# A local-attention stage with its steps in another order, TensorE steps of one tile mode side by side

## The chip, the cores and the metric

The kernel runs on one core of one Trainium2 chip, in float32 (a few tiles of zeros apart). The metric is the device time of one execution in microseconds. A core has five engines, each with its own queue that it works through in order: TensorE (PE; its weight loads are shown apart as PEld), VectorE (DVE), ScalarE (ACT), GpSimd (POOL) and SyncE (SP), which issues the DMAs here. Engines wait for each other by semaphores.

## The reference

Two blocks with adaptive layer norm follow each other on x of 16 x 256 x 128. The first has full attention with 16 heads of 8, and a six-layer local-attention transformer as its second half. The other has a state-space layer and a linear layer. The change is in the six layers:

```python
def attn_layer(x, Wqkv, qs, ksc, Wo):
    qkv = x @ Wqkv
    q, k, v = jnp.split(qkv, 3, -1)
    q, k, v = (sh(q), sh(k), sh(v))          # 16 heads of 64
    q = l2norm(q) * qs
    k = l2norm(k) * ksc
    q = q * cos * scale + rotate_half(q) * sin * scale
    k = k * cos * inv + rotate_half(k) * sin * inv
    out = local_attention(q, k, v)           # windows of 32: own and previous one
    return out @ Wo

def ffn_layer(x, g, bln, W1, b1, W2, b2):
    xn = (x - mu) / jnp.sqrt(var + 1e-05) * g + bln
    a, gate = jnp.split(xn @ W1 + b1, 2, -1)
    return a * jax.nn.gelu(gate, approximate=False) @ W2 + b2

for i in range(DEPTH):                       # 6
    x = attn_layer(shift_tokens(x), Wqkv[i], q_scale[i], k_scale[i], Wo[i]) + x
    x = ffn_layer(shift_tokens(x), ln_g[i], ln_b[i], W1[i], b1[i], W2[i], b2[i]) + x
```

## The kernel before

The kernel has three stages: full attention (about 0 to 431 us), the six layers (431 to 3332 us) and the state-space block with the linear layer (to the end). x is kept transposed, features on partitions, in F.

In the middle stage a group is two sequences (512 tokens); eight groups make one layer and 48 groups the stage. `run` (class `Transformer`) works in 48 periods. In each it goes through ORDER, a list written out by hand of step names with a lag: `Tk10@1` is step T for k, sequence 1, token half 0, of the group that entered one period ago. So up to four groups are in work at once. The list's order is the order of the instructions in each engine's queue, since the stage is recorded under a manual schedule: nothing reorders it. After the 48 periods TAIL does the rest of the last groups, with some steps of the next stage's first group among them (marked `@s`).

The steps, with their engine and, for PE, the tile of the array that the weights take (rows * columns):

- P (L628, PE 128*128): q or k of 128 tokens for all heads, two matmuls of 512 columns. Q (ACT) squares them, C and N (DVE) multiply by cosine and sine, R (DVE) sums the squares, A (POOL) adds the two rotary parts, MXS (POOL), SQ (ACT), RR (DVE) make the norms' inverses, M (POOL) applies them.
- T (L702, PE 64*128): transposes q or k, 16 matmuls of 64 columns. E (ACT) copies the result out.
- K (ACT) writes the mask into PSUM, S (L759, PE 64*32) adds the scores: 64 small float32 products, 128 matmul records and as many weight loads in the profile.
- MX, SB (DVE) find and subtract the maxima, EX (ACT) takes exponentials, SM (DVE) their sums, NR (POOL) divides, TP (DVE) transposes.
- X (PE 128*128), W (ACT), V (SP, two DMAs) lay out x for the values. G (L817, PE 32*128) multiplies the probabilities with x; B (ACT) copies it to `at`, two copies a G.
- Y (L838, PE 128*128): four heads a step through the product of value and output weights. FADD (DVE) adds the result to F.
- F1, F5 (PE transposes), F2 (DVE), F3, FN (POOL), F4, F6 (ACT) are the layer norm; FP (L914, PE), FE (ACT), FM (DVE), FY (L938, PE), FF (DVE) the feed-forward part.
- `value_output` (L608, PE, 64-row weights) makes the product of value and output weights of the next layer, in the last two periods of a layer, and copies it on ACT.

PSUM is handed out by `Slots`: `two` has three places of two banks (P, T, K with S, G twice, FP, the value product), `one` has two places (X, Y, F1, F5, FY). A step that takes a place waits until all that used it before have let it go: a P's place is free after two Q, one C and two N; that of K and S after SB; that of T after E; that of G after B. Other Slots hold the SBUF buffers (`u` seven, `w` four, `pp`, `pT`, `qT` two each). Places go round in the order in which the list frees them.

Of the kernel before, what the change touches and what calls it, by code (L numbers as in the profile page):

```python
# [17 lines left out]
P = 128  # L18
B, S, D = 16, 256, 128
# [3 lines left out]
NG = B // G  # L23
# [435 lines left out]


ORDER = """
Pq00@0 FM2@3 Cq00@0 Nq000@0 EX01@1 Mq10@1 Mk10@1 SM01@1 EX00@1 G10@2 Qq000@0 FADD0@2 B101@2 B100@2
Ak11@1 FY@3 Nq001@0 Aq00@0 SM00@1 Qq001@0 Rq00@0 G11@2 B111@2 FF@3 Mq11@1 X0@1 Pk01@0 Ck01@0 Tk10@1
B110@2 Pq01@0 Nk010@0 Nk011@0 W0@1 Ek10@1 Qk010@0 Cq01@0 Qk011@0 Pk00@0 Ak01@0 Tq10@1 V0@1 Qk000@0
Qk001@0 Nq010@0 Nq011@0 Aq01@0 NR00@1 Y10@2 Eq10@1 Y11@2 Qq010@0 Qq011@0 Rk01@0 Rk00@0 NR01@1 Ck00@0
K10@1 Nk000@0 Rq01@0 MXS0@0 Mk11@1 Tq11@1 Eq11@1 S10@1 Nk001@0 TP00@1 Ak00@0 Pq11@0 MX10@1 SB10@1
SQ0@0 Qq110@0 Nq110@0 Nq111@0 Cq11@0 Pq10@0 Qq100@0 Qq101@0 Tk11@1 Y12@2 Qq111@0 Nq100@0 Nq101@0
Cq10@0 Ek11@1 Y13@2 FADD1@2 G00@1 K11@1 B000@1 S11@1 TP01@1 B001@1 X1@1 G01@1 RR0@0 EX10@1 Aq10@0
MX11@1 Mk00@0 SB11@1 F1@2 F2@2 B010@1 B011@1 Mq00@0 W1@1 EX11@1 Rq10@0 Mq01@0 Pk10@0 Pk11@0 Qk110@0
Tk00@0 Ek00@0 F3@2 FN@2 F4@2 Ck10@0 Nk100@0 Nk101@0 Ck11@0 Aq11@0 V1@1 Y00@1 Tq00@0 Eq00@0 Y01@1  # L470
Tq01@0 F5@2 Qk100@0 Y02@1 Qk101@0 K00@0 SM11@1 F6@2 Mk01@0 SM10@1 S00@0 Eq01@0 Tk01@0 Rk10@0 Nk110@0
Nk111@0 NR11@1 TP11@1 Qk111@0 MX00@0 SB00@0 Ek01@0 FP0@2 FE0@2 Rk11@0 K01@0 FP1@2 NR10@1 Y03@1
Rq11@0 MXS1@0 FE1@2 FM0@2 FM1@2 Ak10@0 SQ1@0 TP10@1 RR1@0 S01@0 MX01@0 FP2@2 FE2@2 SB01@0
"""

TAIL = """
Ak11@0 Mk10@0 X0@0 FADD0@1 Mk11@0 W0@0 G10@1 FM2@2 L1@s B101@1 Mq11@0 G11@1 EX00@0 B110@1 B111@1  # L480
ST@s B100@1 Mq10@0 FY@2 Tq11@0 AG@s Tk10@0 Tk11@0 SM00@0 Eq11@0 Tq10@0 FF@2 Ek10@0 RS@s NB@s Y10@1
K11@0 Ek11@0 EX01@0 Y11@1 NR00@0 S11@0 V0@0 TP00@0 Y12@1 Eq10@0 SM01@0 MX11@0 Y13@1 XN@s L2@s SB11@0
K10@0 G00@0 FADD1@1 X1@0 EX11@0 SM11@0 S10@0 HT@s NR01@0 F1@1 B001@0 TP01@0 MX10@0 SB10@0 B000@0
NR11@0 W1@0 PX1@s U1@s G01@0 B010@0 PX0@s F2@1 B011@0 TP11@0 V1@0 Y00@0 F3@1 EX10@0 FN@1 Y01@0 G11@0
U0@s SM10@0 Y02@0 NR10@0 TP10@0 F4@1 Y03@0 PD@s B111@0 B110@0 XD@s WB@s G10@0 B100@0 B101@0 PZ1@s
F5@1 FADD0@0 ZA1@s F6@1 PZ0@s ZA0@s EE@s WW@s Y10@0 W2@s Y11@0 Y12@0 Y13@0 ZR1@s FADD1@0 FP0@1 F1@0
ZR0@s FP1@1 LL@s FP2@1 FE1@1 LW@s F2@0 FE0@1 F3@0 ZF@s FM1@1 FM0@1 FE2@1 FN@0 DU@s F4@0 FM2@1 F5@0
FY@1 F6@0 FP1@0 FP2@0 FP0@0 FE1@0 FF@1 FE2@0 TB@s FM1@0 FM2@0 FE0@0 FM0@0 FY@0 CB@s FF@0 MS@s
"""


# [20 lines left out]
class Transformer:  # L512
# [460 lines left out]
    def run(self):  # L973
        steps = []
        for o in ORDER.split():
            name, lag = o.split("@")
            base = name.rstrip("0123456789") if name[0] != "F" or name[:2] == "FA" else name
            steps.append((name, int(lag)))
        last = max(lag for _, lag in steps)
        groups = {}  # L980
        n = DEPTH * NG
        for jh in range(2):
            self.value_output(0, jh)
        for p in range(n):
# [722 lines left out]
```

## Time and profile before

| what | value |
|---|---|
| median of 3 runs | 3852.29 us (3850.81 to 3856.6) |
| the profiled execution's span | 3847.4 us, 4.9 below the median |
| mean granted TensorE clock | 0.987 |
| first stage, 0 to 431 us | PE 379, DVE 229, ACT 220, POOL 105 us busy |
| 500 to 3200 us | PE 2668, weight loads 1626, DVE 2548, ACT 2052, POOL 1981 us busy |
| 3330 us to the end | PE 478, DVE 463, ACT 430, POOL 410 us busy |
| matmuls, weight loads | 45040, 45040 |

The profile is of one execution. Its span runs from the first to the last instruction of the program; the profiled execution's own time is given by that span alone, and what lies around it is seen only as the 4.9 us by which the median of the runs is longer. Busy times overlap within an engine by a little, since one instruction's end covers the next one's start; for PE the ends are modelled, so that start to next start tells more than a length.

### The profile page before, as it was taken

The page shows a single profiled execution, that of the slowest core. Times are in us where ns is not written, and L with a number is a line of the kernel's source. Part 1 is how long each engine was busy: PE and PEld are TensorE (multiplying, and loading weights), DVE is VectorE, ACT ScalarE, POOL GpSimd, SP SyncE. Part 2 cuts the span into 40 slices and gives each one's busy share as a digit, 9 for nine tenths or more (in the row PEclk, how much of TensorE's full clock was granted, in tenths as well). Part 3 has the DMA queues.
Part 4 walks back from the last instruction along what each step waited for, and adds up shares of the span by engine and source line. Part 5 has one row for each costly group of instructions (what it writes and reads, how often), then busy time and mean ns, then how long its engine had stood idle before and what let it go on. Part 6 is the DMA issues. An engine that isn't in the chain of part 4 may idle for free.

```text
span 3847.4 us, 104054 instructions
## 1 busy us (share of the span) xinstructions
PE 3693.1 (96%) x45040; PEld 2197.4 (57%) x45040; DVE 3385.9 (88%) x4736; ACT 2820.0 (73%) x4009; POOL 2603.6 (68%) x1636
## 2 busy tenths in 40 slices
PE   8999689999999999999999999999999999899997
PEld 4445355665655656666556656566665556555554
DVE  4665489999999999999999999999999999599997
ACT  3565467777777777777777777777777777689895
POOL 2222477777777777777777777777777776388887
PEclk9999789999999999999999999999999999999999
DMA  1000001000010000100001000010000000243432
GB/s 54 8 7 5 1 7 34 6 5 7 6 34 5 7 6 6 35 6 6 5 7 34 5 6 7 6 34 7 6 6 5 20 7 6 82 117 104 123 109 71
DMA packets 85669, 97.21 MB, mean 25 GB/s; under 512 B 9416, under 2 KB 56668, under 8 KB 84444
## 3 DMA queue, kind: packets, MB, share of 16 engines
q1 hardware_dynamic: 85212, 90.56, 8.5%
q8 instruction: 355, 5.82, 0.6%
q14 instruction: 102, 0.84, 0.1%
HBM read 75.32 MB, written 3.94 MB: 21 GB/s over the span
## 4 chain that ended last, share of the span: by engine, by line
PE 65%; DVE 20%; issue 2%; POOL 1%; ACT 1%; DVEq 0%; POOLq 0%; ACTq 0%
PE py L838 16%; PE pq L628 11%; PE pa L817 7%; PE fp L914 7%; PE s L759 6%; PE pt L702 5%; DVE w L656 3%; PE y L1361 3%; DVE u L644 3%; DVE ss L668 3%; PE db L1345 2%; DVE sm L791 2%; DVE s L1351 2%; PE px L1202 1%; DVE F L951 1%
## 5 line engine op out<-in xcount | busy, mean ns | idle before, releaser
L675 POOL TENSOR_TENSOR u<-u,w 128x1024 f32<-128x1024 f32 x384 | 907.2, 2367 | 405.2 <-DVE w L656 218.3
L690 POOL TENSOR_TENSOR u<-u,r 128x1024 f32<-128x1024 f32 x384 | 724.5, 1903 | 19.1 <-DVE r L686 16.6
L838 PE MATMUL py<-at,wvo 128*128 128x256 f32 x3072 | 736.5, 388 | 0.1
L628 PE MATMUL pq<-wqk,F 128*128 128x512 f32 x1536 | 715.6, 604 | 9.4 <-ACT sq L638 3.3
L638 ACT ACTIVATE sq<-pq 128x512 f32<-128x512 f32 x768 | 432.8, 601 | 301.3 <-PE pq L628 157.3
L838 PEld LDWEIGHTS py<-at,wvo 128*128 128x128 f32 x3072 | 569.6, 192 | 103.2 <-issue 23.2
L644 DVE TENSOR_TENSOR u<-pq,cosl 128x1024 f32<-128x1024 f32 x384 | 466.6, 1215 | 46.2 <-PE pq L628 43.1
L656 DVE TENSOR_TENSOR w<-pq,sinl 128x512 f32<-128x512 f32 x768 | 499.4, 681 | 8.9 <-ACT sq L638 2.1
L828 ACT COPY at<-pa 128x1024 f32<-128x1024 f32 x384 | 368.6, 1012 | 162.9 <-PE pa L817 157.9
L668 DVE TENSOR_REDUCE ss<-sq 128x16 f32<-128x1024 f32 x384 | 451.5, 1196 | 6.2 <-ACT sq L638 6.2
L628 PEld LDWEIGHTS pq<-wqk,F 128*128 128x128 f32 x1536 | 277.0, 191 | 296.2 <-issue 257.2
L817 PE MATMUL pa<-pT,xw 32*128 32x512 f32 x3072 | 411.8, 620 | 5.5 <-ACT sq L638 2.1
L798 POOL TENSOR_TENSOR pp<-pp,sm 128x1024 f32<-128x1024 f32 x192 | 363.8, 1916 | 50.3 <-DVE sm L794 50.3
L702 PEld LDWEIGHTS pt<-ident,u 64*128 64x128 f32 x6144 | 223.7, 139 | 227.0 <-issue 81.8
L1351 DVE TENSOR_TENSOR_SCAN s<-da,db 128x512 f32<-128x512 f32 x256 | 301.1, 1207 | 21.2 <-PE db L1345 9.3
L759 PEld LDWEIGHTS s<-kT,qT 64*32 64x32 f32 x24576 | 257.0, 106 | 90.0 <-issue 79.2
L759 PE MATMUL s<-kT,qT 64*32 64x64 f32 x24576 | 290.3, 227 | 16.4 <-issue 11.3
L702 PE MATMUL pt<-ident,u 64*128 64x64 f32 x6144 | 275.5, 230 | 29.4 <-ACT sq L638 10.6
L772 DVE TENSOR_REDUCE mx<-s 128x16 f32<-128x1024 f32 x192 | 230.5, 1200 | 69.7 <-PE s L759 67.2
L252 DVE TENSOR_REDUCE mx<-s 128x2 f32<-128x512 f32 x256 | 165.3, 687 | 139.9 <-PE sT L280 121.5
L817 PEld LDWEIGHTS pa<-pT,xw 32*128 32x128 f32 x3072 | 180.2, 186 | 172.6 <-issue 76.8
L914 PE MATMUL fp<-hT,w 128*128 128x512 f32 (+1 forms) x576 | 270.7, 606 | 0.0
(223 smaller groups left out, 6269.3 us busy)
## 6 DMA issues: line engine op xcount, KB each, us to landing
btd<-bc SPq DMA_DIRECT2D x72, 512.0 KB
bte<-bc SPq DMA_DIRECT2D x56, 256.0 KB
xw<-xw SPq DMA_DIRECT2D x96, 96.0 KB
wqk<-in_Wqk SPq DMA_DIRECT2D x6, 1024.0 KB
wv<-in_LWvT SPq DMA_DIRECT2D x6, 512.0 KB
wo<-in_Wo SPq DMA_DIRECT2D x6, 512.0 KB
xin<-in_x SPq DMA_DIRECT2D x8, 256.0 KB
out<-ot SPq DMA_DIRECT2D x8, 256.0 KB
```

The costliest lines, as they stand in the source:

```text
L628: nc.tensor.matmul(q.p[:, x], self.F[:, g.b0 + b, o : o + P], g.l.wqk[:, k, x, :], start=True, stop=True)
L638: self.c.nc.scalar.activation(q.sq[:, x], q.p[:, x], AF.Square)
L644: self.c.nc.vector.tensor_tensor(q.u.rearrange("p h x d -> p x h d"), q.p, g.l.cosl[:, t, k].unsqueeze(2).to_broadcast([P, 2, HEADS, DH // ...
L656: self.c.nc.vector.tensor_tensor(q.w[:, :, x], q.p[:, 1 - x], g.l.sinl[:, t, k, x, :].unsqueeze(1).to_broadcast([P, HEADS, DH // 2]), ALU. ...
L668: self.c.nc.vector.tensor_reduce(g.ss[b][:, t, k, :], q.sq.rearrange("p x h d -> p h x d"), AX.XY, ALU.add)
L675: self.c.nc.gpsimd.tensor_tensor(q.u, q.u, q.w, ALU.add)
L690: self.c.nc.gpsimd.tensor_tensor(uf, uf, g.r[b][:, t, k, :].unsqueeze(2).to_broadcast([P, HEADS, DH]), ALU.mult)
L702: self.c.nc.tensor.matmul(q.pt[:, r, j, :], uf[rs, j * P : (j + 1) * P], self.c.ident[rs, rs], is_transpose=True, start=(j == 0), stop=Tru ...
L759: nc.tensor.matmul(s[qs, e, j, :], qT[es, j, qs], kT[es, j, ks : ks + 2 * W], start=False, stop=True, skip_group_check=True,)
L817: self.c.nc.tensor.matmul(g.pa[b, t, w // 2][:, w % 2, :], self.xw[b][qs, t, k, :], g.pT[b, t][qs, k, :], start=(k == 0), stop=(k == 1),)
L838: self.c.nc.tensor.matmul(g.py[b], g.l.wvo[:, h, :], self.at[:, h, :], start=(h == 0), stop=(h == HEADS - 1),)
L914: self.c.nc.tensor.matmul(p[0:n, x, :], g.l.w1[:, w : w + n], g.hT, start=True, stop=True)
```

## The change

ORDER is a new order of the same steps; the cut between two periods is moved (S00, K00, K01, S01 and what follows them now open a period with lag 1 instead of closing it with lag 0). TAIL is new as well; it holds the steps that the moved cut leaves over, and the same early steps of the next stage. `value_output` is split: its matmuls (PW) and its copies (PC) are now steps of the list, where they stood ahead of the list before. Around one period PE's steps change tile mode 29 times in the old order and 21 times in the new one.

PE's steps of the old list, in order: Pq00 G10 FY G11 X0 Pk01 Tk10 Pq01 Pk00 Tq10 Y10 Y11 Tq11 S10 Pq11 Pq10 Tk11 Y12 Y13 G00 S11 X1 G01 F1 Pk10 Pk11 Tk00 Y00 Tq00 Y01 Tq01 F5 Y02 S00 Tk01 FP0 FP1 Y03 S01 FP2.

PE's steps of the new list: S00 S01 FP0 Pq00 Y03 G10 FY Tq10 G11 PW X0 Pk01 Pk00 Pq01 Y10 Tq11 Tk10 Y11 Pq11 Pq10 Y12 S10 Tk11 Y13 G00 S11 F1 X1 G01 Pk10 Tq00 Tq01 Y00 Y01 Tk00 Tk01 F5 Pk11 FP1 FP2 Y02.

```diff
--- before.py
+++ after.py
@@ -459,33 +459,36 @@
 
 
 ORDER = """
-Pq00@0 FM2@3 Cq00@0 Nq000@0 EX01@1 Mq10@1 Mk10@1 SM01@1 EX00@1 G10@2 Qq000@0 FADD0@2 B101@2 B100@2
-Ak11@1 FY@3 Nq001@0 Aq00@0 SM00@1 Qq001@0 Rq00@0 G11@2 B111@2 FF@3 Mq11@1 X0@1 Pk01@0 Ck01@0 Tk10@1
-B110@2 Pq01@0 Nk010@0 Nk011@0 W0@1 Ek10@1 Qk010@0 Cq01@0 Qk011@0 Pk00@0 Ak01@0 Tq10@1 V0@1 Qk000@0
-Qk001@0 Nq010@0 Nq011@0 Aq01@0 NR00@1 Y10@2 Eq10@1 Y11@2 Qq010@0 Qq011@0 Rk01@0 Rk00@0 NR01@1 Ck00@0
-K10@1 Nk000@0 Rq01@0 MXS0@0 Mk11@1 Tq11@1 Eq11@1 S10@1 Nk001@0 TP00@1 Ak00@0 Pq11@0 MX10@1 SB10@1
-SQ0@0 Qq110@0 Nq110@0 Nq111@0 Cq11@0 Pq10@0 Qq100@0 Qq101@0 Tk11@1 Y12@2 Qq111@0 Nq100@0 Nq101@0
-Cq10@0 Ek11@1 Y13@2 FADD1@2 G00@1 K11@1 B000@1 S11@1 TP01@1 B001@1 X1@1 G01@1 RR0@0 EX10@1 Aq10@0
-MX11@1 Mk00@0 SB11@1 F1@2 F2@2 B010@1 B011@1 Mq00@0 W1@1 EX11@1 Rq10@0 Mq01@0 Pk10@0 Pk11@0 Qk110@0
-Tk00@0 Ek00@0 F3@2 FN@2 F4@2 Ck10@0 Nk100@0 Nk101@0 Ck11@0 Aq11@0 V1@1 Y00@1 Tq00@0 Eq00@0 Y01@1
-Tq01@0 F5@2 Qk100@0 Y02@1 Qk101@0 K00@0 SM11@1 F6@2 Mk01@0 SM10@1 S00@0 Eq01@0 Tk01@0 Rk10@0 Nk110@0
-Nk111@0 NR11@1 TP11@1 Qk111@0 MX00@0 SB00@0 Ek01@0 FP0@2 FE0@2 Rk11@0 K01@0 FP1@2 NR10@1 Y03@1
-Rq11@0 MXS1@0 FE1@2 FM0@2 FM1@2 Ak10@0 SQ1@0 TP10@1 RR1@0 S01@0 MX01@0 FP2@2 FE2@2 SB01@0
+K00@1 K01@1 TP11@2 Aq10@1 Rk11@1 FE2@3 MXS1@1 FM2@3 S00@1 S01@1 SQ1@1 Ak10@1 MX00@1 SB00@1 FP0@3
+Pq00@0 MX01@1 FE0@3 RR1@1 EX00@1 FM0@3 Y03@2 SB01@1 EX01@1 SM00@1 Qq000@0 Mq10@1 G10@2 Nq000@0
+Nq001@0 NR00@1 Cq00@0 B101@2 Qq001@0 B100@2 FY@3 Tq10@1 G11@2 SM01@1 Rq00@0 Eq10@1 FADD0@2 FF@3
+B110@2 Ak11@1 TP00@1 PW@0 X0@1 B111@2 Pk01@0 Pk00@0 Ck01@0 Aq00@0 PC@0 W0@1 Mk10@1 Nk010@0 Pq01@0
+Y10@2 Qk000@0 Nk011@0 Mq11@1 Nk000@0 Qk010@0 Qk011@0 Mk11@1 Ck00@0 Qk001@0 Tq11@1 Nk001@0 Tk10@1
+Cq01@0 Rk01@0 Eq11@1 Qq010@0 Ak01@0 Nq010@0 Ek10@1 NR01@1 Rk00@0 Y11@2 Pq11@0 Pq10@0 Y12@2 Nq011@0
+Qq011@0 Qq110@0 K10@1 Rq01@0 Ak00@0 Cq11@0 Aq01@0 Nq110@0 Nq111@0 V0@1 Cq10@0 S10@1 MXS0@0 Nq100@0
+MX10@1 SQ0@0 Qq111@0 Qq100@0 Tk11@1 Nq101@0 Qq101@0 Y13@2 Ek11@1 SB10@1 RR0@0 G00@1 K11@1 S11@1
+FADD1@2 F1@2 B001@1 B000@1 X1@1 TP01@1 EX10@1 MX11@1 SB11@1 Aq11@0 F2@2 G01@1 Mq01@0 B011@1 Pk10@0
+W1@1 Rq10@0 B010@1 Qk100@0 Qk101@0 Mq00@0 V1@1 Mk00@0 Tq00@0 F3@2 SM10@1 Nk100@0 Tq01@0 FN@2 Rk10@0
+EX11@1 Mk01@0 Eq01@0 Eq00@0 Y00@1 Nk101@0 F4@2 Y01@1 Tk00@0 Tk01@0 Ck10@0 Rq11@0 Ek00@0 NR10@1 F5@2
+SM11@1 Pk11@0 F6@2 FP1@2 TP10@1 Ek01@0 NR11@1 Qk110@0 Nk110@0 Ck11@0 FE1@2 FP2@2 FM1@2 Y02@1 Qk111@0
+Nk111@0
 """
 
 
 
 
 TAIL = """
-Ak11@0 Mk10@0 X0@0 FADD0@1 Mk11@0 W0@0 G10@1 FM2@2 L1@s B101@1 Mq11@0 G11@1 EX00@0 B110@1 B111@1
-ST@s B100@1 Mq10@0 FY@2 Tq11@0 AG@s Tk10@0 Tk11@0 SM00@0 Eq11@0 Tq10@0 FF@2 Ek10@0 RS@s NB@s Y10@1
-K11@0 Ek11@0 EX01@0 Y11@1 NR00@0 S11@0 V0@0 TP00@0 Y12@1 Eq10@0 SM01@0 MX11@0 Y13@1 XN@s L2@s SB11@0
-K10@0 G00@0 FADD1@1 X1@0 EX11@0 SM11@0 S10@0 HT@s NR01@0 F1@1 B001@0 TP01@0 MX10@0 SB10@0 B000@0
-NR11@0 W1@0 PX1@s U1@s G01@0 B010@0 PX0@s F2@1 B011@0 TP11@0 V1@0 Y00@0 F3@1 EX10@0 FN@1 Y01@0 G11@0
-U0@s SM10@0 Y02@0 NR10@0 TP10@0 F4@1 Y03@0 PD@s B111@0 B110@0 XD@s WB@s G10@0 B100@0 B101@0 PZ1@s
-F5@1 FADD0@0 ZA1@s F6@1 PZ0@s ZA0@s EE@s WW@s Y10@0 W2@s Y11@0 Y12@0 Y13@0 ZR1@s FADD1@0 FP0@1 F1@0
-ZR0@s FP1@1 LL@s FP2@1 FE1@1 LW@s F2@0 FE0@1 F3@0 ZF@s FM1@1 FM0@1 FE2@1 FN@0 DU@s F4@0 FM2@1 F5@0
-FY@1 F6@0 FP1@0 FP2@0 FP0@0 FE1@0 FF@1 FE2@0 TB@s FM1@0 FM2@0 FE0@0 FM0@0 FY@0 CB@s FF@0 MS@s
+L1@s TP11@1 FE2@2 FM2@2 K00@0 ST@s AG@s Ak10@0 Ak11@0 S00@0 MX00@0 SB00@0 RS@s NB@s K01@0 S01@0 XN@s
+MX01@0 SB01@0 Y03@1 G10@1 B100@1 L2@s HT@s FADD0@1 B101@1 FP0@2 Rk11@0 PX1@s PX0@s FE0@2 MXS1@0
+SQ1@0 U1@s FM0@2 RR1@0 Mk10@0 X0@0 W0@0 U0@s G11@1 B110@1 X1@0 Aq10@0 Mq10@0 W1@0 PD@s B111@1 XD@s
+Tk10@0 Ek10@0 Tq10@0 EX01@0 SM01@0 PZ0@s ZA0@s ZR0@s Mk11@0 PZ1@s ZA1@s Y10@1 Y11@1 Y12@1 Mq11@0
+V0@0 NR01@0 ZR1@s EX00@0 SM00@0 NR00@0 Eq10@0 K10@0 Tk11@0 Ek11@0 Tq11@0 Eq11@0 TP01@0 S10@0 TB@s
+G01@0 TP00@0 Y13@1 MX10@0 CB@s V1@0 FY@2 SB10@0 EX10@0 B011@0 WB@s FADD1@1 B010@0 K11@0 G00@0 B000@0
+S11@0 B001@0 F1@1 SM10@0 FF@2 Y00@0 Y01@0 EE@s MX11@0 NR10@0 TP10@0 SB11@0 EX11@0 F2@1 Y02@0 Y03@0
+WW@s LL@s SM11@0 F3@1 FN@1 F4@1 G10@0 B100@0 F5@1 W2@s F6@1 NR11@0 TP11@0 B101@0 G11@0 B110@0 LW@s
+FP2@1 ZF@s B111@0 Y10@0 Y11@0 Y12@0 DU@s MS@s FE2@1 FM2@1 FADD0@0 Y13@0 FP0@1 FE0@1 FADD1@0 F1@0
+F2@0 F3@0 FP1@1 FM0@1 FE1@1 FM1@1 FY@1 FN@0 F4@0 F5@0 F6@0 FP2@0 FP1@0 FE1@0 FF@1 FM1@0 FE2@0 FP0@0
+FE0@0 FM2@0 FM0@0 FY@0 FF@0
 """
 
 
@@ -599,7 +602,7 @@
         nc, l = self.c.nc, self.layers[i]
         if jh == 0:
             l.wvo = self.wp.tile([P, HEADS, D], F32, tag="wvo", name="wvo")
-        pw = self.two.take([P, 2, 4, D], "pw")
+        pw = l.pw = self.two.take([P, 2, 4, D], "pw")
         for j in range(4):
             for e in range(2):
                 es = slice(e * DH, (e + 1) * DH)
@@ -613,6 +616,11 @@
                     stop=True,
                     skip_group_check=True,
                 )
+
+    def value_output_copy(self, i, jh):
+
+        nc, l = self.c.nc, self.layers[i]
+        pw = l.pw
         for e in range(2):
             o = e * PAIRS + jh * 4
             nc.scalar.copy(l.wvo[:, o : o + 4, :], pw[:, e])
@@ -981,17 +989,20 @@
         n = DEPTH * NG
         for jh in range(2):
             self.value_output(0, jh)
+            self.value_output_copy(0, jh)
         for p in range(n):
             i, j = divmod(p, NG)
             if j == last + 1 and i + 1 < DEPTH:
                 self.load(i + 1)
-            if j >= NG - 2 and i + 1 < DEPTH:
-                self.value_output(i + 1, j - NG + 2)
             if p == n - 4:
                 self.early.load()
             groups[p] = self.group(p)
             for name, lag in steps:
-                if p >= lag:
+                if name in ("PW", "PC"):
+                    if j >= NG - 2 and i + 1 < DEPTH:
+                        value = self.value_output if name == "PW" else self.value_output_copy
+                        value(i + 1, j - NG + 2)
+                elif p >= lag:
                     self.step(name, groups[p - lag])
             groups.pop(p - last, None)
         for o in TAIL.split():
```

## The prediction, made before the run

> **What bounds the kernel now.** I read the engines' shares first, then a stretch of about one period, then TensorE's own timeline, then the waits.
>
> ```profile
> PE 3693.1 (96%) x45040; PEld 2197.4 (57%) x45040; DVE 3385.9 (88%) x4736; ACT 2820.0 (73%) x4009; POOL 2603.6 (68%) x1636
> PE   8999689999999999999999999999999999899997
> DVE  4665489999999999999999999999999999599997
> ```
> ```profile
> 1380.00:1438.20 58.20, 57.81 (x830) 35.09 (x830) 55.74 (x76) 44.77 (x58) 43.24 (x26) 1.00 0.02 6
> ```
>
> The first fence is the page, the second the busy time in 1380 to 1438.2 us, about one period: PE 57.81, weight loads 35.09, DVE 55.74, ACT 44.77, POOL 43.24, at full granted clock. PE is nearest to full and DVE second by 2 us. Busy time alone would not settle it, so I looked at whether PE's starts follow each other without idle time:
>
> ```profile
> 2336.46 3.65 PE L628 MATMUL pq<-wqk,F 128*128 128x512 f32 x8
> 2340.04 0.71 PE L702 MATMUL pt<-ident,u 64*128 64x64 f32 x16
> 2340.68 2.00 PE L838 MATMUL py<-at,wvo 128*128 128x256 f32 x8
> 2342.61 0.71 PE L702 MATMUL pt<-ident,u 64*128 64x64 f32 x16
> 2343.25 2.00 PE L838 MATMUL py<-at,wvo 128*128 128x256 f32 x8
> 2345.17 0.71 PE L702 MATMUL pt<-ident,u 64*128 64x64 f32 x16
> ...
> 2373.68 0.71 PE L702 MATMUL pt<-ident,u 64*128 64x64 f32 x16
> 2374.32 3.72 PE L838 MATMUL py<-at,wvo 128*128 128x256 f32 x16
> 2377.97 0.71 PE L702 MATMUL pt<-ident,u 64*128 64x64 f32 x16
> 2378.61 1.29 PE L759 MATMUL s<-kT,qT 64*32 64x64 f32 x105
> 2380.10 0.43 PE L759 MATMUL s<-kT,qT 64*32 64x64 f32 x23 [0.20 <-issue]
> ```
> ```profile
> PE s L759 <- issue: 9.5, 9, 1.8
> PE pt L702 <- DVE pp L778: 4.8, 21, 0.2
> ```
> ```profile
> DVE mx L772 <- PE s L759: 51.6, 72, 1.8
> DVE u L644 <- PE pq L628: 22.8, 39, 1.5
> ```
>
> The columns of the timeline are start, length, engine, line. Every step starts as the one before lets go; the waits (second fence: total us, times, longest, over 39 periods from 600 to 2900 us) are small. DVE's largest waits are for PE (third fence). So in these periods PE's queue sets the time. FY starts at 2007.49 and, 16 periods on, at 2947.88: 58.8 us a period. Adding the shortest start-to-start time of each run of steps over one period gives 57.4, so some 1.4 us a period are waits.
>
> **The change part by part.** Nothing is computed more or less; only orders change. What a visit to another tile mode costs is in the fence above, as start to next start. One visit of Y with 4 heads among T steps takes 1.93 (2340.68 to 2342.61). One visit with 8 heads takes 3.65 (2374.32 to 2377.97), not 3.86. So each visit of a 128*128 run carries 0.21 us that does not grow with its work. A T among others takes 0.64 (2377.97 to 2378.61). T steps side by side stand in the trace once, in the last groups:
>
> ```profile
> 3261.73 1.71 PE L702 MATMUL pt<-ident,u 64*128 64x64 f32 x48
> ```
>
> Three take 1.71 where one takes 0.71, so a further T costs 0.50 and each T visit saved is worth 0.14.
>
> Counted from the order around one period, the old one has 29 visits: 13 of 128*128 (Pq00 with FP2; FY; X0 Pk01; Pq01 Pk00; Y10 Y11; Pq11 Pq10; Y12 Y13; X1; F1 Pk10 Pk11; Y00; Y01; F5 Y02; FP0 FP1 Y03), 8 of T, 4 of S, 4 of G. The new one has 21: 9 of 128*128, 5 of T (Tq11 Tk10, Tq00 Tq01, Tk00 Tk01 in pairs), 3 of S (S00 S01 side by side), 4 of G.
> - Four 128*128 visits: 4 x 0.21 = 0.84.
> - Three T visits: 3 x 0.14 = 0.42.
> - One S visit: two S steps never stand together in the trace. The bounds are +0.14, as T, and a loss of the 1.8 that an S waited at most for instructions; I take +0.10, near T, and keep the loss for the range.
> - Sum 1.36 us a period, so PE needs about 56.0.
>
> The first periods of the stage are not full (the fifth and sixth slices of PE); I count 46 of 48: 46 x 1.36 = 62.6.
>
> PW moves from between FP2 and Pq00 to between G11 and X0, where it splits no 128*128 visit: 0.2 x 10 times = 2. PC's two copies go to ACT behind B111 instead of ahead of the period; ACT is 44.8 of 58.2 busy there, and PE asks for PW's bank only some steps later: nothing. The rotation (K00, K01, S00, S01 and FP0 now open a period) moves work from the last loop round into TAIL: no cost by itself. The last groups have the same steps and early steps. Laid end to end by these rows, PE from S00 of the last group to its Y13 is some 2 us shorter beyond the moved steps, and the chain behind Y13 (FADD, F1 to FF, 22 us from 3309.7) stays. I take 2, with 6 either way.
>
> What hides the other queues: each engine has the same instructions a period, ACT also the same six table loads by the order of its functions. POOL keeps its 24 steps, 43 us, with 15 idle. SP keeps its four xw transfers: W0 to G00 were 19 us apart (2014.15 to 2033.16), and are still some 17 by PE's rows. DVE keeps 55.7 us of work; against 56.0 it has far less slack than against 57.4, and this is the cover that gets thin.
>
> I laid PE's new order end to end and asked at each step what must be ready, with the rows' lengths. Tightest: S11 needs K11's copy, behind MX10, Nq101 and SB10: 1.6 (S to MX, 2035.34 to 2036.93) + 1.2 + 0.6 + 1.15 + 1.03 and some 0.15 of handing over, 5.7 us from S10's start, with 5.9 of PE work between (S10 1.41, Tk11 0.64, Y13 1.93, G00 1.93). Pk10 needs the bank of SB11: nothing to spare. G00 needs Nq101's bank, F5 needs four F4 on ACT, S00 needs K00 behind FM1: 0.2 to 0.4 to spare each. No missing piece of a microsecond shows. I therefore leave the 1.4 us of waits as they are. Bounds: half of them go, to the 0.7 that the old order's shortest period (58.1) has over 57.4, which is 46 x 0.7 = 33 us more gained; or the five tight places cost 0.15 each on top, 35 us less.
>
> Sum: 62.6 + 2 + 2 = 66 us less. The profiled span is 3847.4, and 3781 after; the runs' median is 3852.3, 5 above the span, so **3786 us**.
>
> One rule speaks against this. The Trainium skill, Perfetto Trace Analysis, Identifying the Most-Contended Engine, says that matmul busy time is no good measure of TensorE's headroom and that the share of the weight loads is. By it PE would be 35.09 of 58.20 full, 60%, DVE with 96% the engine to work on, and this change worth nothing: 3852. I go by the starts that follow each other and by DVE's waits for PE instead.
>
> **The rivals.**
> - *Instructions arrive late at the paired S (slower).* PE's instructions come in 16 KB pieces, 355 for 90,080 matmuls and weight loads, some 256 in each, which is about what one S issues in 1.41 us. When a piece is late, PE stops inside or right behind an S:
>
> ```profile
> 3213.18 1.44 PE L759 MATMUL s<-kT,qT 64*32 64x64 f32 x123
> 3216.03 0.31 PE L759 MATMUL s<-kT,qT 64*32 64x64 f32 x5 [1.41 <-issue]
> ```
> ```profile
> q8 instruction: 355, 5.82, 0.6%
> ```
>
> S00 S01 side by side run through two pieces in 2.8 us in every period. If each pair stops for the longest wait seen, 1.8: 47 x 1.8 = 85 lost, 66 gained, 3871. It decides from 1.6 us a pair. Against it: the long stops stand behind T then S (Tq11 S10), where PE's queue had nothing slow to run ahead of; the new order has no T right before an S, and Y02, 1.8 us, goes before S00. Many S run through a border with no stop. I expect 0.2 to 0.4 a pair, about what is lost now.
> - *The tight places bind (smaller gain).* DVE becomes a second bound at 55.7 plus its own waits. At 57.5 us a period the gain is 46 x 0.7 + 4: about 3816.
> - *DVE's waits stay whole (no change).* If its 2.5 idle us of 58.2 remain, the period stays 58.2 to 58.8 and the time near 3850. Against it: these waits are for PE steps that now come earlier.
> - *The pairing doesn't save what it says.* If the pairs cost as much as apart, as S may, only the 128*128 visits count: 46 x 0.84 + 4 = 43, 3809.
>
> **How the numbers follow.** Forecast, 3745 to 3804: 0.62. Smaller gain, from DVE, tight places or half-saved switches, 3804 to 3844: 0.21. No change, within 0.2% (8 us, about what a measurement of this kernel tells): 0.05. Slower by the S pair or a stall I missed: 0.12, up to 3880. So faster 0.83, same 0.05, slower 0.12. The range leaves out the slower cases, no change and the last of the smaller gains, and below it the case that more than the 33 us of waits goes: 3750 to 3838. The likeliest one's own range is 3750 to 3804.
>
> **What would show it.** In the profile after: FY to FY near 57.4; paired T of 32 matmuls in 1.2 us; Y of 16 between single T visits 3.65; two S in 2.8. DVE busy near 98% in the steady slices, with less wait of MX for S. Wrong: a gap inside S00 S01 over 1 us in most periods ("issue" ahead of s), PE waiting for SB, K or FM by 0.5 us or more each period, or the last groups longer than before by 10 us.

## The result: 5% slower, and the profile after

The changed kernel takes 4041.85 us (median of 4 runs, 4035.35 to 4045.29), the kernel before 3851.55 in the same comparison: a ratio of 1.0495, 95% interval 1.048 to 1.051. Forecast were 66 us less; it became 190 more.

Where the 195 us between the two profiled spans lie is read from the starts of FY, one for each of the 48 groups:

| stretch | before | after | difference |
|---|---|---|---|
| start to the first FY | 595.5 | 604.3 | +8.8 |
| 40 periods from there | 2352.3 (58.8 each) | 2500.0 (62.5 each) | +147.7 |
| last seven FY to FY | 379.5 | 417.3 | +37.8 |
| behind the last FY | 520.1 | 520.8 | +0.7 |

So the steady period lost 3.7 us where 1.4 had been promised as gain, and the last seven lost more than seven times that. On the page (busy us, share, then the 40 slices) no engine is as full as before; PE falls from 96% to 92%, DVE from 88% to 84%:

```profile
PE 3704.4 (92%) x45040; PEld 2195.7 (54%) x45040; DVE 3395.6 (84%) x4736; ACT 2818.7 (70%) x4007; POOL 2604.5 (64%) x1636
PE   8999589999999999999999999999998989899997
DVE  5654588888898888888899888888888988589997
```

One period (start:end, length, then PE, PEld, DVE, ACT, POOL busy) has the old work in a longer time, at full clock:

```profile
2043.76:2105.62 61.86, 57.95 (x834) 35.11 (x830) 55.52 (x76) 44.78 (x58) 43.11 (x25) 1.00 0.02 6
```

The pairs themselves do what was said. TensorE's timeline of the changed kernel (start, length, line):

```profile
2080.25 1.21 PE L710 MATMUL pt<-ident,u 64*128 64x64 f32 x32
2081.39 3.72 PE L846 MATMUL py<-at,wvo 128*128 128x256 f32 x16
2085.04 1.21 PE L710 MATMUL pt<-ident,u 64*128 64x64 f32 x32
```

Two T take 1.14 from start to next start (0.64 + 0.50), two Y 3.65. Adding the shortest start-to-start time of each run of steps (where a step waits in every period, its length from a run below in which it doesn't) gives 55.9 us a period, against 57.4 before: the 1.4 of the forecast is there. What replaced it are waits. PE's and DVE's waits from 600 to 2900 us (total, times, longest):

```profile
PE s L767 <- issue: 64.0, 35, 2.4
PE pt L710 <- ACT sq L646: 42.8, 37, 1.2
PE pa L825 <- ACT sq L646: 25.8, 37, 0.7
PE pt L710 <- DVE w L664: 11.8, 24, 0.5
```
```profile
DVE act L933 <- ACT act L926: 57.7, 73, 2.6
DVE w L664 <- ACT sq L646: 54.8, 77, 0.8
DVE ss L676 <- ACT sq L646: 24.6, 37, 0.7
```

In the 37 periods of that stretch S waits 1.7 us a period for instructions (before: 9.5 us in 39), T and G 2.2 for a ScalarE or VectorE reader (before: 4.8 us in all 39). `DVE w <- ACT sq` is a strange line: N writes w from P's PSUM tile and a table, and never touches sq. Before, that line stood at 0.6 us. Two places in the timeline show both kinds. First the pair S00 S01, the step FP0 behind it:

```profile
2094.76 1.15 PE L767 MATMUL s<-kT,qT 64*32 64x64 f32 x91
2097.68 0.73 PE L767 MATMUL s<-kT,qT 64*32 64x64 f32 x50 [1.76 <-issue]
2098.34 1.98 PE L922 MATMUL fp<-hT,w 128*128 128x512 f32 x4
```

Then ScalarE, VectorE and TensorE in turn, from Nq110 Nq111 to G00:

```profile
2065.90 1.28 DVE L664 TENSOR_TENSOR w<-pq,sinl 128x512 f32<-128x512 f32 x2
2067.21 0.60 ACT L646 ACTIVATE sq<-pq 128x512 f32<-128x512 f32 x1 [0.64 <-DVE w L664]
2067.95 0.71 PE L710 MATMUL pt<-ident,u 64*128 64x64 f32 x16 [0.90 <-ACT sq L646]
2068.23 0.68 DVE L664 TENSOR_TENSOR w<-pq,sinl 128x512 f32<-128x512 f32 x1
2068.83 1.22 DVE L780 TENSOR_REDUCE mx<-s 128x16 f32<-128x1024 f32 x1
2069.00 0.60 ACT L646 ACTIVATE sq<-pq 128x512 f32<-128x512 f32 x1 [1.19 <-DVE w L664]
2069.96 0.68 DVE L664 TENSOR_TENSOR w<-pq,sinl 128x512 f32<-128x512 f32 x1
2070.67 0.60 ACT L646 ACTIVATE sq<-pq 128x512 f32<-128x512 f32 x1 [1.07 <-DVE w L664]
2071.17 1.01 ACT L727 COPY kT<-pt 128x1024 f32<-128x1024 f32 x1
2071.32 2.89 PE L825 MATMUL pa<-pT,xw 32*128 32x512 f32 x16 [0.73 <-ACT sq L646]
```

The reader is to see a zigzag. Qq111 (2067.21) starts when Nq111 ends, though both only read Pq11; Tk11, which takes that place, waits for it. Then Qq100 waits for Nq100, MX10 goes in between on VectorE, Qq101 waits for Nq101, Ek11 stands behind Qq101 on ScalarE, and G00 needs both their places. The readers of a P tile (two Q, one C, two N) are handed over in the order of the list whenever the engine changes. The new list changes engine two or three times on six of its eight tiles, 18 times a period; the old list has 12 changes, and just one on five of the eight. The last wait, inside G00, isn't in the list of waits: by start to next start G00 takes 2.82 in every period where 1.93 is its shortest, since its later matmuls need the place that Ek11 lets go.

### The profile page after: what moved, and what is told of

It is laid out like the page before. It is cut to its first block, busy times and chain, and to the rows that moved or that the text cites. A ratio compares the mean times of both kernels' runs of the same rounds, so it can differ in the third digit from the quotient of the medians.

```text
span 4042.4 us, 104103 instructions
## 1 busy us (share of the span) xinstructions
PE 3704.4 (92%) x45040; PEld 2195.7 (54%) x45040; DVE 3395.6 (84%) x4736; ACT 2818.7 (70%) x4007; POOL 2604.5 (64%) x1636
## 4 chain that ended last, share of the span: by engine, by line
PE 45%; DVE 32%; ACT 7%; issue 4%; POOL 1%; DMA 0%; DVEq 0%; POOLq 0%; ACTq 0%; SPq 0%
DVE w L664 8%; DVE u L652 8%; PE py L846 7%; PE pa L825 7%; PE fp L922 7%; PE pq L636 5%; DVE ss L676 5%; PE s L767 5%; PE y L1372 3%; ACT sq L646 3%; PE pt L710 3%; DVE sm L799 2%; PE db L1356 2%; DVE F L959 2%; DVE s L1362 2%
## 5 line engine op out<-in xcount | busy, mean ns | idle before, releaser
L646 ACT ACTIVATE sq<-pq 128x512 f32<-128x512 f32 x768 | 443.0, 598 | 503.2 <-DVE w L664 279.7
L676 DVE TENSOR_REDUCE ss<-sq 128x16 f32<-128x1024 f32 x384 | 461.0, 1201 | 32.8 <-ACT sq L646 32.7
L836 ACT COPY at<-pa 128x1024 f32<-128x1024 f32 x384 | 379.2, 1013 | 152.8 <-PE pa L825 152.7
L636 PEld LDWEIGHTS pq<-wqk,F 128*128 128x128 f32 x1536 | 287.4, 195 | 338.6 <-issue 308.1
L825 PE MATMUL pa<-pT,xw 32*128 32x512 f32 x3072 | 429.3, 619 | 32.7 <-ACT sq L646 32.1
L710 PE MATMUL pt<-ident,u 64*128 64x64 f32 x6144 | 258.5, 231 | 106.9 <-ACT sq L646 73.2
L922 PE MATMUL fp<-hT,w 128*128 128x512 f32 (+1 forms) x576 | 287.9, 638 | 5.9 <-DVE mx L780 2.1
L1372 PE MATMUL y<-hc,ident 128*128 128x512 f32 x512 | 245.8, 606 | 19.0 <-POOL hc L1366 17.2
```

The source lines that it names most:

```text
L636: nc.tensor.matmul(q.p[:, x], self.F[:, g.b0 + b, o : o + P], g.l.wqk[:, k, x, :], start=True, stop=True)
L646: self.c.nc.scalar.activation(q.sq[:, x], q.p[:, x], AF.Square)
L676: self.c.nc.vector.tensor_reduce(g.ss[b][:, t, k, :], q.sq.rearrange("p x h d -> p h x d"), AX.XY, ALU.add)
L710: self.c.nc.tensor.matmul(q.pt[:, r, j, :], uf[rs, j * P : (j + 1) * P], self.c.ident[rs, rs], is_transpose=True, start=(j == 0), stop=Tru ...
L825: self.c.nc.tensor.matmul(g.pa[b, t, w // 2][:, w % 2, :], self.xw[b][qs, t, k, :], g.pT[b, t][qs, k, :], start=(k == 0), stop=(k == 1),)
L922: self.c.nc.tensor.matmul(p[0:n, x, :], g.l.w1[:, w : w + n], g.hT, start=True, stop=True)
```

## The experiments

Theory 1: the loss is this hand-over between ScalarE's and VectorE's reads of one PSUM tile. Theory 2: it is instructions that arrive late inside S00 S01 (the prediction's first rival). Theory 3: PE's new order is slow by itself. "Period" below is the mean of the same 40 FY to FY, "tail" the last seven.

| run | median us | ratio to before, 95% interval | period | tail |
|---|---|---|---|---|
| changed kernel | 4041.9 | 1.0495 (1.048 to 1.051) | 62.5 | 417.3 |
| e1_readers | 3948.0 | 1.0254 (1.0234 to 1.0273) | 60.6 | 404.1 |
| e2_s_apart | 3966.9 | 1.0300 (1.0283 to 1.0317) | 60.8 | 410.0 |
| e3_both | 3879.8 | 1.0077 (1.0062 to 1.0092) | 59.0 | 402.0 |
| refit | 3972.1 | 1.0314 (1.0298 to 1.0331) | 61.0 | 406.5 |
| refit_apart | 3901.1 | 1.0132 (1.0110 to 1.0154) | 59.4 | 402.7 |
| half_s01 | 3954.3 (one run) | | 60.5 | 408.7 |
| both_xt | 3850.1 | 0.9998 (0.9985 to 1.0011) | 58.9 | 374.1 |
| resort | 3849.9 | 0.9995 (0.9985 to 1.0005) | 58.4 | 401.7 |
| resort_xt | 3814.3 | 0.9908 (0.9888 to 0.9929) | 58.3 | 366.3 |
| unpair | 3821.8 | 0.9924 (0.9909 to 0.9939) | 58.6 | 366.3 |
| resort2 | 3787.4 | 0.9838 (0.9822 to 0.9854) | 57.6 | 370.0 |
| before | 3851.6 | 1 | 58.8 | 379.5 |

**e1_readers: four ScalarE steps moved.**

```diff
-Y10@2 Qk000@0 Nk011@0 Mq11@1 Nk000@0 Qk010@0 Qk011@0 Mk11@1 Ck00@0 Qk001@0 Tq11@1 Nk001@0 Tk10@1
+Y10@2 Qk000@0 Qk001@0 Nk011@0 Mq11@1 Nk000@0 Qk010@0 Qk011@0 Mk11@1 Ck00@0 Tq11@1 Nk001@0 Tk10@1
...
-Qq011@0 Qq110@0 K10@1 Rq01@0 Ak00@0 Cq11@0 Aq01@0 Nq110@0 Nq111@0 V0@1 Cq10@0 S10@1 MXS0@0 Nq100@0
-MX10@1 SQ0@0 Qq111@0 Qq100@0 Tk11@1 Nq101@0 Qq101@0 Y13@2 Ek11@1 SB10@1 RR0@0 G00@1 K11@1 S11@1
+Qq011@0 Qq110@0 Qq111@0 K10@1 Rq01@0 Ak00@0 Cq11@0 Aq01@0 Nq110@0 Nq111@0 V0@1 Qq100@0 Qq101@0
+Cq10@0 S10@1 MXS0@0 Nq100@0 MX10@1 SQ0@0 Tk11@1 Nq101@0 Y13@2 Ek11@1 SB10@1 RR0@0 G00@1 K11@1 S11@1
```

> The changed kernel with four steps of ScalarE's list moved and nothing else: Qk001 goes right behind Qk000, Qq111 right behind Qq110, and Qq100 and Qq101 ahead of Cq10, so that on three PSUM tiles ScalarE's two reads come before VectorE's three. TensorE's order, VectorE's order, the pairs and the last groups stay. Theory 1 (reads of one PSUM tile by ScalarE and VectorE wait for each other in the order of the list, and the new list alternates them): the waits of Tk11 (1.2 us), of G00 (0.7 and 1.1) and of the three VectorE steps behind a square (0.6 to 0.8 each) mostly go, 1.8 us a period of 61.9, 46 x 1.8 = 83 us: about 3958, between 3930 and 3985. Theory 2 (all of the loss is instructions late inside S00 S01): no change, 4042. Theory 3 (TensorE is slower in its new order by itself): no change.

Measured: 94 us less. The four moves take the changes of engine from 18 to 13 a period. Of PE's waits, that for late instructions is whole, the others are about halved:

```profile
PE s L767 <- issue: 68.1, 36, 2.4
PE pa L825 <- DVE w L664: 26.0, 36, 0.7
PE pt L710 <- DVE w L664: 11.1, 38, 0.3
```

Theory 1 holds, with its size; theories 2 and 3 alone would have left 4042.

**e2_s_apart: S01 behind FP0.**

```diff
-K00@1 K01@1 TP11@2 Aq10@1 Rk11@1 FE2@3 MXS1@1 FM2@3 S00@1 S01@1 SQ1@1 Ak10@1 MX00@1 SB00@1 FP0@3
+K00@1 FE2@3 K01@1 TP11@2 Aq10@1 FM2@3 Rk11@1 MXS1@1 S00@1 SQ1@1 Ak10@1 MX00@1 SB00@1 FP0@3 S01@1
```

> The changed kernel with S01 moved from behind S00 to behind FP0, so that two matmul steps of 512 columns stand between the two S; FE2 and FM2 of the older group go a few places earlier, since FP0 needs their bank. Theory 2 (instructions arrive late inside the pair, 1.7 us in nearly every period): the stop inside the pair goes, one more S visit and a short wait of FP0 for FM2 come, 1.6 us a period less, 46 x 1.6 = 74: about 3968, between 3945 and 3990; the row 's waits on issue' falls from 64 us to under 15. Theory 1 alone (the stop in the pair is hidden behind the waits between ScalarE and VectorE): under 20 us less, 4025 or more.

Measured: 75 us less, and the stop is gone:

```profile
PE pt L710 <- ACT sq L646: 44.6, 38, 1.2
PE pa L825 <- ACT sq L646: 26.9, 38, 0.7
PE pt L710 <- DVE w L664: 18.6, 28, 0.7
PE s L767 <- issue: 0.9, 4, 0.3
```

FE2 and FM2 moved too, and VectorE's wait for FE falls from 57.7 us to 6.8. That it is S01 which carries the gain is shown by refit_apart below, where S01 alone is moved.

**e3_both: the two edits together.**

> Both edits of the two runs above together. If they are two separate losses on the path, they add: 3.4 us a period, 46 x 3.4 = 156, about 3886, between 3850 and 3920. If one hides the other, the time is that of the better of the two alone, near 3960.

Measured: 162 us less; 94 and 75 add up to 169. They are two separate losses on the path, and together they are most of the steady loss against the kernel before: 62.5 falls to 59.0 a period, with PE's order changed by one step only.

**refit: PE's order kept, the other engines' steps in another order.** The list is new as a whole; the part around the tiles of e1 became

```diff
+Cq01@0 Tq11@1 Eq11@1 Tk10@1 W0@1 Qq010@0 Y11@2 Qq011@0 Rk01@0 Nq010@0 Nq011@0 Ek10@1 Rq01@0 Pq11@0
+K10@1 Ak00@0 Pq10@0 Y12@2 NR01@1 V0@1 Nq110@0 S10@1 Nq111@0 Aq01@0 MXS0@0 Qq100@0 Cq11@0 Qq110@0
...
```

> The changed kernel with TensorE's order exactly as it is, S00 S01 side by side included, and the steps of ScalarE, VectorE and GpSimd put in another order around it, so that on each PSUM tile the two engines hand over once and no step asks for what comes much later. Theory 1: the period falls from 61.9 to about 57.5 with the stop inside the pair still there, 46 x 4.4 = 200 us less, about 3842, between 3800 and 3890. Theory 3 (the new TensorE order is the loss): 4000 or more. Theory 2 alone: no change, 4042.

A miss: 3972.1, 70 less instead of 200. The list does not quite do what the expectation says: counted in it, Pq00 changes engine four times, Pq10 three times and Pq01 twice, 14 changes in all. Its stops in the pair were as long as ever, and other places began to wait, among them G00 and F5:

```profile
PE s L767 <- issue: 74.4, 51, 2.4
PE pa L825 <- DVE pp L786: 13.3, 38, 0.4
PE f L902 <- ACT xn L890: 13.1, 22, 0.6
```

By start to next start, S00 S01 took 4.78 where 2.66 is the shortest, FP0 behind it 2.43 instead of 1.82. FP0 shows a second cost of the stop. In 24 of 40 periods it takes 1.82; in the other 16 it takes 2.8 to 3.5, and there the granted clock is 0.50 for 3.4 us. Two such places, first the windows (the clock is the third number from the end), then FP0 in them:

```profile
1999.50:2002.90 3.40, 3.40 (x77) 2.02 (x56) 3.37 (x4) 2.04 (x2) 1.90 (x1) 0.50 0.02 5
2061.40:2064.80 3.40, 3.39 (x32) 1.70 (x32) 3.37 (x4) 3.00 (x4) 1.90 (x1) 1.00 0.00 0
```
```profile
2000.51 3.16 PE L922 MATMUL fp<-hT,w 128*128 128x512 f32 x4
2061.77 1.98 PE L922 MATMUL fp<-hT,w 128*128 128x512 f32 x4
```

The changed kernel has 12 such periods, the kernel before and e2_s_apart none. So I took S01 out of the pair there too.

**refit_apart: refit with S01 behind FP0.**

> The run refit (TensorE's order of the changed kernel, the other engines' steps put in another order) came to 3972 instead of 3842; its trace shows S00 with S01 at 4.78 us a period where 2.66 is its shortest, and FP0 behind it at 2.43 where 1.82 is its shortest. This kernel is refit with one step moved: S01 goes from behind S00 to behind FP0. If the late instructions in the pair, and what they push back, are why refit missed (2.1 + 0.6 in the pair and most of the 0.4 to 0.9 at Tk00 Tk01, Pk11 and G00 behind it): 61.0 falls to about 57.6 a period, 46 x 3.4 = 156 less, about 3816, between 3790 and 3860. If the loss of refit lies elsewhere (VectorE's or GpSimd's order), only the 1.6 a period that the same move gave to the changed kernel goes, 3972 - 75 = 3897, or less.

Measured: 3901, 71 less; the second reading. The pair costs 71 to 75 us in both orders, and refit's missing rest was in my order of the other engines: taking G10, G00, F5 and Pk11 over their shortest lengths, some 1.7 us a period remain that I hadn't counted.

**half_s01: half of S01's matmuls left out.**

```diff
-        for j in range(PAIRS):
+        for j in range(PAIRS // 2 if (b, t) == (0, 1) else PAIRS):
```

> The changed kernel with half of the matmuls of S01 left out (four of its eight head pairs), everything else as it is; half of one attention score tile of each sequence's group is not computed. S00 S01 then issue 384 instead of 512 matmuls and weight loads, 1.5 pieces of 256 instead of two. If the stop inside the pair is the wait for the next piece of instructions, it stands no longer in most periods or gets shorter: the row 's waits on issue' falls from 64 us in 37 periods to under 40, while the time falls by the 0.7 us of matmuls and the shorter stop, 46 x 1.2 = 55 or more: 3990 or less. If the stop has to do with S01 itself (its bank, its operands), it stays at 1.7 a period and the time falls by 0.7 x 46 = 32: about 4010.

Measured: 3954.3 (one run), 88 less, and the stops fall from 35 to 15:

```profile
PE s L767 <- issue: 24.4, 15, 2.1
```

In 25 of 40 periods the pair now takes 2.04 us without a stop. The first reading holds: the stop goes with how much the pair issues, not with S01's bank or operands. The trace of the changed kernel says when. Its instruction queue brings 355 pieces; 34 times a stop of over 0.6 us falls inside an S between 600 and 2900 us, and each time PE goes on 2.3 to 2.9 us after the start of the last piece. One S is 128 matmuls and 128 weight loads, about one piece, and lasts 1.41 us. As I read it, a second S at once has used up its piece before the next is there; the trace shows the times, not the buffer.

**both_xt: the last layer's additions moved.** The tail is 402 us in e3_both against 379.5 before, though the periods are alike. Looking for it, I compared the groups of VectorE there: the four additions into xT at the end of FF (only in the last layer) take 5.4 us instead of 1.9. GpSimd and VectorE in the changed kernel, then in the kernel before:

```profile
3110.28 5.98 POOL L698 TENSOR_TENSOR u<-u,r 128x1024 f32<-128x1024 f32 x3
3111.32 5.74 DVE L968 SCALAR_TENSOR_TENSOR xT<-F,m0mod,xT 64x256 f32<-64x256 f32 x4
```
```profile
2953.20 1.91 POOL L690 TENSOR_TENSOR u<-u,r 128x1024 f32<-128x1024 f32 x1
2955.19 2.02 DVE L960 SCALAR_TENSOR_TENSOR xT<-F,m0mod,xT 64x256 f32<-64x256 f32 x4
```

```diff
         self.one.drop(g.f)
+
+    def FX(self, g):
+        nc = self.c.nc
         if g.layer == DEPTH - 1:
...
-SM11@1 Pk11@0 F6@2 FP1@2 TP10@1 Ek01@0 NR11@1 Qk110@0 Nk110@0 Ck11@0 FE1@2 FP2@2 FM1@2 Y02@1
+FX@3 SM11@1 Pk11@0 F6@2 FP1@2 TP10@1 Ek01@0 NR11@1 Qk110@0 Nk110@0 Ck11@0 FE1@2 FP2@2 FM1@2 Y02@1
```

> The run e3_both, with the four xT additions at the end of FF taken out of FF into a step of their own, FX, which stands ahead of SM11 (in TAIL right behind FF). They are done in the last layer alone. In the changed kernel the four take 1.15, 2.01, 2.01 and 0.48 us while GpSimd runs its M steps, five times over; in the kernel before they take 0.48 each, with GpSimd idle. Theory 4 (an xT addition, which reads both its inputs from SBUF, waits for the GpSimd instruction that is under way): in the new place, where GpSimd waits for SM11, they take about 0.48 again, 5 x 3.45 = 17 us less than e3_both: about 3863, between 3855 and 3872. Rival: their length comes with the last layer and not with GpSimd, no change from 3880.

Measured: 3850.1, 30 less, more than the 17 and below the range. The additions are short again, where GpSimd waits:

```profile
3059.29 1.95 DVE L971 SCALAR_TENSOR_TENSOR xT<-F,m0mod,xT 64x256 f32<-64x256 f32 x4
3062.93 1.91 POOL L806 TENSOR_TENSOR pp<-pp,sm 128x1024 f32<-128x1024 f32 x1 [5.57 <-DVE sm L802]
```

Theory 4 holds for the additions' length; resort below has them at 2.42 to 2.61 and 2.47 us behind GpSimd steps of some 2.36. But each of the first four groups of the last layer gives back about 5 us and the fifth 7.5, not 3.45. The trace of e3_both shows a cost that comes on top. In each of the five groups with long additions TensorE stands still for 5.0 us, for a ScalarE step that waits for VectorE, and around its end the granted clock is 0.50 for 6.8 us. Two T then take 2.22 us where they took 1.21 in the changed kernel's timeline above:

```profile
3043.30:3050.10 6.80, 5.90 (x41) 4.93 (x42) 6.07 (x8) 3.31 (x5) 6.31 (x3) 0.50 0.01 2
```
```profile
3044.20 2.22 PE L710 MATMUL pt<-ident,u 64*128 64x64 f32 x32 [5.01 <-ACT sq L646]
```

In both_xt these five waits are gone; over the last seven FY to FY the mean granted clock is 0.99, in e3_both 0.95.

With these three repairs the new order is as fast as the old one, within 0.15%, and no faster. Its saved visits are still eaten by waits: from 600 to 2900 us TensorE waits 44 us in both_xt for an N or for K's copy, 1.1 us a period.

**resort, resort_xt, unpair, resort2.** The last four are new lists for all engines, made by the rules that the runs gave: S steps apart, few hand-overs for each P tile, and (not in resort) xT where GpSimd is idle, still with pairs of T. The second rule, one hand-over a tile, is not kept: counted, resort and resort_xt change engine 14 times a period, with two or three changes on five tiles, and resort2 13 times. So these runs don't test it strictly. Of resort_xt:

```diff
+K00@1 S00@1 TP11@2 FP0@3 Aq10@1 FE2@3 FM2@3 Rk11@1 K01@1 MXS1@1 MX00@1 SB00@1 Ak10@1 SQ1@1 S01@1
+FE0@3 Y03@2 MX01@1 EX00@1 SB01@1 FM0@3 RR1@1 Pq00@0 Nq000@0 Nq001@0 X0@1 Mk10@1 SM00@1 G10@2 Mq10@1
...
+FP1@2 Nk101@0 NR10@1 Qk110@0 FX@3 SM11@1 Rq11@0 TP10@1 Qk111@0 FP2@2 Nk110@0 FE1@2 NR11@1 Ck11@0
```

> The changed kernel's steps with every engine's order put together anew by three rules that the first runs gave: S00 and S01 apart (FP0 between them), each PSUM tile handed over once between ScalarE and VectorE, and TensorE's pairs kept (Tk10 Tq11, Tq01 Tq00, Tk00 Tk01, Y01 F5, Pk01 Pk00). The rows' lengths laid end to end with those waits give 56.1 us a period; e3_both came out 0.7 over what the same sum gave it, so 56.8: 2.0 under the kernel before, 46 x 2.0 = 92, with the last groups some 17 + 5 over it as in e3_both: 3851 - 92 + 22 = 3781, between 3755 and 3830. If TensorE's new pairs can't be fed by VectorE (55.4 us of work) at all, the period stays at 58.5 or more, 3865 or more.

> The run resort, with the xT additions as the step FX ahead of SM11, as in both_xt. By theory 4 again 17 us less than resort: about 3764 if resort is 3781; the same as resort by its rival.

resort came to 3849.9, a miss by 69: its periods were 58.4, not 56.8. The tail had its xT waits, 22 over the kernel before, as expected. resort_xt came to 3814.3: 36 less, again more than 17, and again with the clock: over the last seven FY to FY it is 0.95 in resort and 1.00 in resort_xt. It is the first order here that beats the kernel before.

unpair takes two pairs apart:

```diff
-Y10@2 Nk011@0 Qk000@0 Qk001@0 Ck00@0 Nk000@0 Qk011@0 Ak01@0 Pq01@0 Tk10@1 Nk001@0 Tq11@1 Rk00@0
-Y11@2 Qq010@0 Nq010@0 Ek10@1
+Y10@2 Nk011@0 Qk000@0 Qk001@0 Ck00@0 Nk000@0 Qk011@0 Ak01@0 Pq01@0 Tk10@1 Y11@2 Nk001@0 Tq11@1 Rk00@0
+Qq010@0 Nq010@0 Ek10@1
...
-Eq00@0 F4@2 Tk00@0 EX11@1 Nk100@0 Ck10@0 Ek00@0 Tk01@0 Ek01@0 Rk10@0 Y01@1 F5@2
+Eq00@0 F4@2 Tk00@0 Y01@1 EX11@1 Nk100@0 Ck10@0 Ek00@0 Tk01@0 Ek01@0 Rk10@0 F5@2
```

> resort_xt (3814) with two of TensorE's pairs taken apart again and no other step moved: Y11 goes between Tk10 and Tq11, Y01 between Tk00 and Tk01. That is two more visits of T and two more of 128*128, 2 x 0.14 + 2 x 0.21 = 0.70 us of TensorE a period. If the visits' cost reaches the end time, as the prediction's sum had it, 46 x 0.7 = 32 us more: about 3846. If VectorE (55.4 of work and its waits) sets the period by now, the visits are hidden behind it: 3814 to 3824.

Measured: 7.5 us more (3818.6 to 3825.0 against 3814.0 to 3815.0), in the range of the second reading: of 0.70 us a period of TensorE's time only some 0.2 to 0.3 reach the end. But the starts don't bear out its reason, that VectorE hides the visits everywhere. From Tk00 to the end of Y02, unpair takes 0.25 us a period more (10.72 against 10.47), so most of that pair's 0.35 does reach the end. From Tk10 to S10 both take 8.9. There the pair of resort_xt had saved nothing by itself: in every period Tq11, right behind Tk10, starts 0.15 us after VectorE's Nk001 has ended, so that the pair takes 1.49 from start to next start where Tk00 Tk01 takes 1.14:

```profile
1423.42 1.56 PE L710 MATMUL pt<-ident,u 64*128 64x64 f32 x32
1447.50 1.21 PE L710 MATMUL pt<-ident,u 64*128 64x64 f32 x32
```

Y11 put between the two covers that wait. What hides a visit here is one wait for VectorE at one place; whether TensorE or VectorE sets the rest of the period, no run here separates.

> Another order made by the same rules as resort_xt, with 0.1 us more counted for each wait of TensorE on another engine; TensorE's pairs are Tq11 Tk10, Tq01 Tq00, Y00 Y01 F5, Tk00 Tk01. By the rows' lengths 56.3 us a period as against 56.4 for resort_xt: the same time within 20 us, 3795 to 3835, since both came out some 1.7 over their sum.

Measured: 3787.4, 27 less than resort_xt, a miss on the good side of its range; why it beats its sum I did not follow up. Its page, a period from 2006 us on, and PE's and VectorE's waits from 600 to 2900 us:

```profile
PE 3636.0 (96%) x45040; PEld 2171.0 (57%) x45040; DVE 3376.0 (89%) x4736; ACT 2816.8 (74%) x4007; POOL 2602.2 (69%) x1636
```
```profile
2006.00:2063.60 57.60, 57.48 (x841) 35.22 (x842) 55.77 (x76) 45.07 (x60) 45.15 (x29) 1.00 0.18 54
```
```profile
PE pt L710 <- issue: 2.8, 5, 0.8
PE s L767 <- issue: 1.4, 5, 0.4
```
```profile
DVE mx L780 <- PE s L767: 38.4, 79, 1.0
DVE w L664 <- ACT sq L646: 17.3, 53, 0.9
```

PE has almost no waits in the list, VectorE 1.6 us a period; PE's steps still take over 1 us a period more than their shortest, as before the change. This is the state that the prediction had described: 57.6 us a period (forecast 57.4), 3787 us in all (forecast 3786). It is another list, though: S00 and S01 stand apart, it has 23 visits instead of 21. It does not show that the predicted order itself can run so, and that the totals meet this closely is partly luck.

## Why the prediction was wrong, step by step

- *What bounds the kernel before*: it fits. A list with less PE time and no new waits for PE (resort2) is faster by about that time. VectorE is close behind in both: in resort2 its 55.77 us of work and 1.6 of waits nearly fill the same 57.6.
- *The price of the visits*, 1.36 us a period: right in size, 57.4 to 55.9 of PE's undisturbed time. That it all reaches the end was not: in unpair the saving of one pair of two is lost to a wait for VectorE. "The cover that gets thin" was seen, and rival 2 priced it too low, since it took VectorE's waits as they were. It also counted its gain from 58.2 where the forecast counts from 58.8, so that its 57.5 a period is nearly the forecast's own.
- *"No missing piece of a microsecond shows"*: this step failed. I laid out PE's order against VectorE's steps and let every read of a P tile start when its engine was free. The trace shows that a Q and an N or C on one tile wait for each other in the order of the list. Tk11, G00 and Tk10 each stand behind such a row of hand-overs: where the prediction gave G00 0.2 to 0.4 us to spare, T and G waited 2.2 us a period. e1 prices four moved steps at 94 us. That the 1.4 us of waits stay as they are was the term that this made wrong.
- The Trainium skill, PSUM — Partial Sum Buffer, section on bank collisions, states that two engines on one bank and the same partitions, reads included, must be kept apart, and that the compiler's back end adds a dependency between them. The page speaks against my step. Here the trace shows more than the rule asks: Nk001 reads the tile's first bank and still waits 0.67 us for Qk001, which reads the second; there the hand-over goes by the whole tile of two banks. What puts these waits into the program, no run here shows.
- *The first rival, late instructions at the paired S*: it came true at its own price (1.7 us of waits a period, 71 to 75 us by e2 and refit_apart; 85 was the forecast), and I gave it a chance of 0.12 together with all stalls that I might have missed. The sign that it named, a gap of over 1 us inside the pair in most periods, is there. The reason against it failed: I looked at what stands before the pair, where the count of instructions inside it decides. My 0.2 to 0.4 a pair was what the single S steps of a period lose (9.5 us in 39 periods), and none of those has another S behind it.
- *Last groups*, 2 less, 6 either way: wrong. The last seven FY to FY grew by 38 us; 26 of that is seven times the steady 3.7, but e3_both, with periods as before, still has 22. I looked at PE's and the final chain, not at what GpSimd does while the last layer's xT additions run. With these moved (both_xt) the tail is 374.1 against 379.5. The Trainium skill, SBUF — State Buffer, section on the two separate sides, has the rule: a VectorE instruction with two SBUF inputs and a GpSimd instruction that reads SBUF share a port that one of them holds for its whole instruction. The rows agree: 2.01 us for an addition of 0.48 behind a GpSimd step of 1.9.
- *The rule weighed against*, that the weight loads' share (60%) leaves TensorE room and the change is worth nothing: resort2 speaks for my reading: it is 1.6% faster than the kernel before with VectorE's work unchanged, and its loads' share is 61% (35.22 of 57.60) while PE has almost no waits.
- *Rivals 3 and 4*: neither; the pairs of T and Y save what they say where nothing waits inside them, and VectorE's waits did not stay, they grew.
- *The range* is given once from 3745 and once from 3750; the bound of 33 us under 3786 makes it 3753.

## What to carry to other kernels

An order that saves time on the bounding engine is only as good as the slack of all the others in that very order: lay out every engine's queue with every wait the program will put in, the order of two engines' reads of one PSUM tile too, before pricing the gain. Where a step is made of very many short instructions, don't put two side by side; a slower step between them (here FP0, 1.9 us) lets the instructions arrive. Look at the parts that only the last layer or the last groups do with the same care as at the steady state. Where TensorE stands still for some microseconds, look at the granted clock behind it too.

## What the runs showed of the hardware that was not expected

- TensorE's instruction supply: after a stop PE goes on 2.3 to 2.9 us after a piece of some 256 instructions starts to come. Of two S steps side by side, each using about a piece in 1.41 us, the second stops for it in nearly every period (35 stops in 37); with half a step less most stops are gone (15).
- The granted clock fell to 0.50 for 3.4 us in 16 of 40 periods of refit, each with a stop of 1.8 to 2.4 us in the pair, and for 6.8 us at each of e3_both's five waits of 5.0 us in the last layer.
- FP0, four matmul records in 1.9 us, is enough between two S to take the wait for instructions from 64.0 us to 0.9.
- A VectorE addition of 0.48 us with both inputs in SBUF took 2.01 behind GpSimd steps of 1.9 and 2.47 behind steps of 2.36 (resort), and 0.48 with GpSimd idle. FF's other additions, which read PSUM and SBUF, took 0.48 in both places.
